# Layer 1 of a two-layer cross-attention: eleven of sixteen rotary chains transposed by VectorE in 32x32 blocks that DMA puts in place

## The chip, the cores and the metric

The kernel runs on one core of a Trainium2 chip. It is one launch in float32. The metric is the device time of the launch in microseconds (us): 2907.1 is the median of three runs (2905.81 to 2908.67).

A core has a TensorE (matrix products, results in PSUM), a VectorE, a ScalarE and a GpSimd (called PE, DVE, ACT and POOL in the profile), and SyncE (SP), which here only issues DMAs. Each engine works through its own queue in order, and waits on semaphores for the others.

## The reference

Four sequences of 1024 tokens with 512 features attend, twice, to a context of 1024 tokens with 384 features.

```python
# layer 0: 16 heads of 64
h = layernorm(x) * gamma + beta
Q, K, V = h @ Wq, context @ Wk, context @ Wv
x = x + (softmax(Q K^T) * 64**-0.5) V @ Wo + bo
# layer 1: 16 heads of 32
xn = x * rsqrt(mean(x * x) + 1e-5) * norm_w
q, k, v = xn @ wq, split(context @ wkv)
q, k = rotate(q, cos, sin), rotate(k, cos, sin)       # per head of 32
q, k = q / max(|q|, 1e-12), k / max(|k|, 1e-12)       # per head of 32
x = x + softmax(sqrt(32) * q k^T) v @ wout
```

The change is in layer 1 alone: in how the rotated and normalised q and k, made with tokens in partitions, come to have features in partitions, which the score product needs.

## The kernel before

The four sequences (batches) are worked one after the other. Layer 0 walks over eight pairs of heads; its softmax blocks are transposed by VectorE in 32x32 blocks (L401), and sixteen DMAs per block then put the 32-row bands in place (`regroup`, L407 to L413). Layer 1 works in two halves of eight heads, 256 features each. Each half has 32 steps of `Attention1.step` (L571): four query blocks of 256 tokens, two groups of four heads, four steps over the keys. A step makes scores for four heads and 256 keys on TensorE (L581), exponentials on ScalarE (L591), sums of exponentials on VectorE (L600, L602), and on TensorE the product of the step before with the values (L626). The denominators are added up by a product with ones in the second step of the next block (L645), and the quotient is formed by `divide` (L638, L639).

Queries and keys of layer 1 come from chains (`rotated_chains`, L452). A chain handles two tiles of 128 tokens and the 256 features of a half. Its three parts:

- `project` (L463): matmuls into a PSUM bank, 128 tokens by 256 features for each of the two tiles;
- `rotate` (L475), started by the last matmul: ScalarE squares the bank (L478), VectorE makes three products with cos and sin and adds them (L480 to L483), sums the squares per head (L485), and GpSimd makes the reciprocal norms and multiplies (L487 to L491). The result `t1` lies in one of four slots of a scratch tile, used in turn;
- `turn_over` (L494): four TensorE transposes of 128x128 into a PSUM bank (L499), and one ScalarE copy into the tile of q or k (L504).

Per batch there are sixteen chains: four each for k of half 0 (`k1_b_0`), q of half 0 (`q1_b_0`), k of half 1 and q of half 1. In this document q[0] to q[3] and k[0] to k[3] are those of half 0, and q1[0] to q1[3] and k1[0] to k1[3] those of half 1. All of k and q[0] are made before the steps of half 0 begin, and also k1[0] and the projection of k1[1]. The rest is woven between the steps of half 0: the units of a list are taken out by `Units.fill`, which spreads their costs (L828 to L859). In that list a chain's turn stands two places behind its projection (`weave`, lag 2), and `work.until(marks[n])` (L884) makes sure that q[1], q[2] and q[3] are turned before steps 8, 16 and 24, which read them first. The values of half 1 (`value_chains`, L536) are made in the same list. At the end of half 0 the rest of the list is emptied, so all of q1 and k1 is turned when half 1 begins at step 32. There the two loads of `wout` (L655) are issued by SP in program order, and after them the loads for the next batch; the first unit in step 32 is a product with `wout` (L165).

Both halves of the list run with matmuls that are split into four of 32 output columns once the steps have begun (`which["cols"]`, L832); in layer 0 they are split in two. PSUM banks for these units are given out in turn by `bank` (L127). A unit's cost (0.45 for a turn) only sets how the units are spread.

All loads and stores but three are issued by SP (`nc.sync`), in order. Each DMA uses one of eight semaphores in turn, and waits, before it is issued, for the DMA eight before it.

Of the kernel before, what the change touches and what calls it, by code (L numbers as in the profile page):

```python
# [30 lines left out]
AF = mybir.ActivationFunctionType  # L34
# [3 lines left out]
P = 128  # L38
S = 1024
NT = S // P  # L40
DQ = 512
NQ = DQ // P
DC = 384
NC_ = DC // P
# [4 lines left out]
HD1 = 32  # L49
NGRP = DQ // P  # L50
FH = DQ // 2
# [58 lines left out]
def xattn_kernel(ctx: ExitStack, tc: tile.TileContext, a: dict, out: bass.AP):  # L110
    nc = tc.nc
    x, c = a["x"], a["ctx_768"]
# [325 lines left out]
    TH = 2  # L438
# [10 lines left out]
        nc.sync.dma_start(wq, a["wq"][:, f0:f1].rearrange("(n p) m -> p n m", p=P))  # L449
        return wq  # L450

    def rotated_chains(dst, src, nk, w, name, tmp):  # L452

        hd, nh = HD1 // 2, TH * FH // HD1
        tiles = {}

        def heads(ap):
            return ap.rearrange("p (t h d) -> p t h d", t=TH, d=HD1)

        def spread(ap):  # L460
            return ap.unsqueeze(2).to_broadcast([P, TH, FH // HD1, ap.shape[2]])

        def project(t0, i, k):  # L463
            if i == 0 and k == 0:
                tiles[t0] = [bank(f"{name}_p{t0}")]
                if which["from"] == 0:
                    which["kept"] = which["n"]
            pp = tiles[t0][0]
            t = t0 + i
            lhsT = src[t // 4][:, k, (t % 4) * P : (t % 4 + 1) * P]  # L470
            matmul(pp[:, i * FH : (i + 1) * FH], lhsT, w(k), k == 0, k == nk - 1)
            if i == TH - 1 and k == nk - 1:
                rotate(t0, pp)

        def rotate(t0, pp):  # L475

            t1, t2, sq = tmp.take()
            nc.scalar.activation(sq, pp, AF.Square)  # L478
            c_, s_ = cos[:, t0 : t0 + TH, :], sin[:, t0 : t0 + TH, :]
            nc.vector.tensor_mul(heads(t1), heads(pp), spread(c_))  # L480
            nc.vector.tensor_mul(heads(t2)[:, :, :, :hd], heads(pp)[:, :, :, hd:], spread(s_[:, :, :hd]))
            nc.vector.tensor_mul(heads(t2)[:, :, :, hd:], heads(pp)[:, :, :, :hd], spread(s_[:, :, hd:]))
            nc.vector.tensor_add(t1, t1, t2)  # L483
            ss = sb.tile([P, nh], F32, tag="ss", bufs=2, name=f"{name}_s{t0}")
            nc.vector.tensor_reduce(ss, sq.rearrange("p (h d) -> p h d", d=HD1), AX.X, ALU.add)  # L485
# [5 lines left out]
            nc.gpsimd.tensor_mul(t1h, t1h, ri.unsqueeze(2).to_broadcast([P, nh, HD1]))  # L491
            tiles[t0] = t1

        def turn_over(t0):  # L494
            t1 = tiles.pop(t0)
            pt = bank(f"{name}_t{t0}")
            for g in range(2):
                for i in range(TH):
                    nc.tensor.transpose(  # L499
                        pt[:, (g * TH + i) * P : (g * TH + i + 1) * P],  # L500
                        t1[:, i * FH + g * P : i * FH + (g + 1) * P],
                        ident,
                    )
            nc.scalar.copy(dst()[:, :, t0 * P : (t0 + TH) * P], pt.rearrange("p (g t) -> p g t", g=2))  # L504

        return [
            (
                [(0.44, lambda t0=t0, i=i, k=k: project(t0, i, k)) for i in range(TH) for k in range(nk)],
                [],
                [(0.45, lambda t0=t0: turn_over(t0))],  # L510
            )
            for t0 in range(0, NT, TH)
        ]
# [19 lines left out]
            self.n += 1  # L533
            return self.t[:, self.n % 4], self.t[:, 4 + self.n % 2], self.t[:, 6 + self.n % 2]

    def value_chains(v, wv, ct, name):  # L536
        def one(t0, i, k, st={}):
            if i == 0 and k == 0:
                st["pp"] = bank(f"{name}_{t0}")
            t = t0 + i  # L540
            lhsT = ct[t // 4][:, k, (t % 4) * P : (t % 4 + 1) * P]
            matmul(st["pp"][:, i * FH : (i + 1) * FH], lhsT, wv[:, k, :], k == 0, k == NC_ - 1)
# [10 lines left out]
    WQ = 256  # L553

    class Attention1:
# [61 lines left out]
        def product(self):  # L617
# [15 lines left out]
            if end:  # L633
# [2 lines left out]

                def divide():
                    nc.vector.reciprocal(s[:, 1, :], s[:, 1, :])  # L638
                    nc.vector.tensor_mul(o[g][:, qb * WQ : (qb + 1) * WQ], s[:, 0, :], s[:, 1, :])  # L639

                def sums():
                    for i in (par, 3):
# [85 lines left out]
    for b in range(B):  # L728
# [92 lines left out]
        begin("q")  # L821
        kT, qT = kq["k"], kq["q"]
        kT1, qT1 = qk_tile(f"k1_{b}_1"), sb.tile([P, 2, S], F32, tag="raw", bufs=1, name=f"q1_{b}_1")
        q = rotated_chains(lambda kq=kq: kq["q"], xnT, NQ, lambda k, wq=wq: wq[0][:, k, :], f"q1_{b}_0", tmp)
        k1 = rotated_chains(lambda kT1=kT1: kT1, ct, NC_, lambda k, wk1=wk1: wk1[0][:, k, :], f"k1_{b}_1", tmp)
        q1 = rotated_chains(lambda qT1=qT1: qT1, xnT, NQ, lambda k: wq1[:, k, :], f"q1_{b}_1", tmp)

        work.add(flat(outs[:4]) + norms[0]["stats"] + k1[0][0] + [(AV, att.product)] + norms[0]["apply"])  # L828
        work.add(norms[0]["turn"] + q[0][0] + k1[1][0] + k1[0][2] + [(AV, att.product)] + flat(outs[4:]) + q[0][2])
# [14 lines left out]
        for half in range(2):  # L844
            n = 0
            if half == 0:
                vs = value_chains(att1.v1, wv1, ct, f"pv1_{b}_1")
                first = [q[1], (norms[1]["stats"], [], []), vs[0], (norms[1]["apply"], [], k1[1][2]), k1[2]]
                rest = [(norms[1]["turn"] + q[2][0], [], q[2][2]), k1[3], q[3], q1[0], vs[1], q1[1], q1[2]]
                rest += [q1[3], vs[2], vs[3]]  # L850
# [91 lines left out]
```

## Time and profile before

| | |
|---|---|
| median of three runs | 2907.1 us (2905.81 to 2908.67) |
| the profiled execution, its own time | 2903.3 us |
| its span | 2901.5 us |
| granted TensorE clock, mean | 0.999 |
| layer 1 half 0, first batch (steps 0 to 31) | 497 to 624 us of the span |
| layer 1 half 1, first batch (steps 32 to 63) | 624 to 755 us |
| TensorE transposes of the chains (L499) | 256, median 273 ns each, pipelined |
| ScalarE copies behind them (L504) | 64, some 590 ns each |

The profile is one execution, taken by the hardware profiler. Its page gives the busy time of each engine, the chain of work that ended last, and the groups of instructions by source line. Other views give an engine's instructions in order of time, merged where equal ones follow each other, with the idle time before them and what ended it in brackets; one line's instructions with their least, median and greatest durations in ns; and busy times in chosen stretches. Times in such rows are us from the span's start. A matmul of the source appears as two in the profile. `SPq` is SP's queue of DMA issues; a wait in it stands in the time of the issue.

### The profile page before, as it was taken

What the parts mean: (1) busy time and instruction counts of PE and PEld (TensorE: products, weight loads), DVE (VectorE), ACT (ScalarE), POOL (GpSimd) and SP (SyncE); (2) the same over time, 40 slices, a digit from 0 to 9 for tenths busy, and PEclk for the clock granted to TensorE, in tenths of its full rate; (3) what the DMA queues carried; (4) which work ended last, traced back from release to release, by engine and by line L of the source; (5) the groups of instructions that cost most, each with busy time, mean ns of one, the idle gap of its engine ahead of it and who ended that gap; (6) DMA issues with size and microseconds to landing.
All of it is one profiled execution on the core that took longest, in us unless ns stands there. A gap on an engine that the chain in (4) does not pass through costs nothing.

```text
span 2901.5 us, 66687 instructions
## 1 busy us (share of the span) xinstructions
PE 2849.7 (98%) x27336; PEld 1425.7 (49%) x27336; DVE 2189.1 (75%) x2952; ACT 1439.5 (50%) x2329; POOL 938.9 (32%) x776
## 2 busy tenths in 40 slices
PE   8999999999999999999999999999999999999998
PEld 4444455555444444555544445455554444445544
DVE  5677785877777778587777777858877777786877
ACT  4444444666444444466644444446664444444665
POOL 2343353420134335432024433534102343353400
PEclk9999999999999999999999999999999999999999
DMA  5887775010398777401039887730104887773000
GB/s 144 189 187 181 167 171 133 22 37 25 75 210 192 183 170 175 113 22 36 26 92 211 192 184 166 178 93 22 36 26 112 207 197 183 165 171 81 2 2 30
DMA packets 177552, 348.87 MB, mean 120 GB/s; under 512 B 37600, under 2 KB 93152, under 8 KB 177248
## 3 DMA queue, kind: packets, MB, share of 16 engines
q1 hardware_dynamic: 175920, 343.96, 50.1%
q8 instruction: 216, 3.54, 0.5%
q14 instruction: 88, 0.72, 0.1%
q10 hardware_dynamic: 1328, 0.66, 0.1%
HBM read 67.64 MB, written 8.39 MB: 26 GB/s over the span
## 4 chain that ended last, share of the span: by engine, by line
PE 89%; DVE 4%; ACT 3%; issue 2%; SPq 1%; DMA 1%; POOL 1%; DVEq 0%; ACTq 0%
PE s L367 16%; PE av L428 15%; PE po L165 11%; PE s L581 9%; PE pv L165 8%; PE pqT L165 7%; PE av L626 7%; PE pkT L165 5%; PE q_p L165 4%; PE k_p L165 2%; PE av L645 2%; ACT e L591 1%; SPq L412 1%; PE pth L247 1%; DMA eT<-e 1%
## 5 line engine op out<-in xcount | busy, mean ns | idle before, releaser
L392 DVE TENSOR_REDUCE m<-s 128x1 f32<-128x1024 f32 x512 | 602.9, 1219 | 372.1 <-PE s L367 371.5
L591 ACT ACTIVATE e<-s 128x1024 f32<-128x1024 f32 x512 | 496.7, 1022 | 252.5 <-PE s L581 239.5
L398 POOL TENSOR_SCALAR raw<-raw,li 128x1024 f32<-128x1024 f32 x256 | 287.1, 1122 | 725.0 <-DVE li L397 717.0
L367 PE MATMUL s<-qk 64*128 64x512 f32 x2048 | 515.6, 615 | 2.9 <-ACT e L393 2.2
L393 ACT ACTIVATE e<-s,m 128x1024 f32<-128x1024 f32 x256 | 283.1, 1110 | 465.8 <-DVE m L392 224.2
L393 ACT ACTIVATE raw<-s,m 128x1024 f32<-128x1024 f32 x256 | 285.4, 1115 | 455.0 <-DVE m L392 455.0
L428 PE MATMUL av<-eT,v 128*64 128x256 f32 x4096 | 470.1, 382 | 4.8 <-DMA eT<-e 3.6
L398 POOL TENSOR_SCALAR e<-e,li 128x1024 f32<-128x1024 f32 x256 | 287.0, 1122 | 473.7 <-DVE li L397 244.2
L600 DVE TENSOR_TENSOR both<-e 128x512 f32<-128x512 f32 x512 | 340.5, 699 | 87.2 <-ACT e L591 84.3
L428 PEld LDWEIGHTS av<-eT,v 128*64 128x64 f32 x4096 | 284.7, 137 | 225.1 <-issue 84.8
L367 PEld LDWEIGHTS s<-qk 64*128 64x128 f32 x2048 | 183.7, 186 | 281.6 <-issue 165.9
L581 PE MATMUL s<-q,k 32*128 32x256 f32 x4096 | 306.0, 401 | 5.8 <-ACT q L504 2.7
L401 DVE STREAM_TRANSPOSE e<-e 128x1024 f32<-128x1024 f32 x256 | 310.0, 1229 | 0.3
L401 DVE STREAM_TRANSPOSE e<-raw 128x1024 f32<-128x1024 f32 x256 | 310.0, 1228 | 0.2 <-DMA eT<-e 0.2
L581 PEld LDWEIGHTS s<-q,k 32*128 32x128 f32 x4096 | 192.1, 184 | 141.0 <-ACT e L591 72.0
L165 PE MATMUL pqT<-hT,w 128*64 128x512 f32 (+1 forms) x1216 | 240.6, 595 | 2.5 <-ACT hT L249 2.5
L165 PE MATMUL po<-wo,vals 128*64 128x512 f32 x1024 | 234.6, 596 | 0.0
L295 DVE TENSOR_TENSOR x<-x,po 128x512 f32<-128x512 f32 x200 | 131.7, 678 | 86.2 <-PE po L165 85.2
L165 PEld LDWEIGHTS pv<-w,cT 128*64 128x64 f32 (+1 forms) x3360 | 170.3, 132 | 41.6 <-issue 34.8
L165 PE MATMUL pv<-w,cT 128*64 128x128 f32 (+1 forms) x3360 | 184.3, 274 | 0.7 <-ACT hT L249 0.7
L165 PE MATMUL pkT<-cT,w 128*64 128x512 f32 (+1 forms) x912 | 182.4, 598 | 0.0
L602 DVE TENSOR_TENSOR both<-both 128x1024 f32<-128x1024 f32 x128 | 159.7, 1248 | 4.4
(82 smaller groups left out, 2776.1 us busy)
## 6 DMA issues: line engine op xcount, KB each, us to landing
eT<-e SPq DMA_DIRECT2D x2048, 128.0 KB, 2.4
xr<-in_x_dram SPq DMA_DIRECT2D x32, 256.0 KB, 4.0
wo<-in_Wo_dram SPq DMA_DIRECT2D x16, 512.0 KB, 4.5
x<-in_x_dram SPq DMA_DIRECT2D x32, 256.0 KB, 4.0
out_dram<-x SPq DMA_DIRECT2D x32, 256.0 KB, 2.6
w<-in_Wq_dram SPq DMA_DIRECT2D x31, 256.0 KB, 3.2
c<-in_ctx_dram SPq DMA_DIRECT2D x32, 192.0 KB, 4.2
wkv<-in_wkv_dram SPq DMA_DIRECT2D x16, 384.0 KB, 3.5
```

The source lines that it names most:

```text
L165: nc.tensor.matmul(o[rr], lhsT[:, rr], rhs, start=start, stop=stop)
L367: nc.tensor.matmul(sc[j][:, kb * 512 : (kb + 1) * 512], pr["qT"][r[j], i * P : (i + 1) * P], pr["kT"][r[j], kb * 512 : (kb + 1) * 512], st ...
L392: nc.vector.tensor_reduce(m[:, j : j + 1], sc[j], AX.X, ALU.max, negate=True)
L393: nc.scalar.activation(e[j], sc[j].rearrange("p (g s) -> p g s", g=4), AF.Exp, bias=m[:, j : j + 1], accum_out=l[:, j : j + 1])
L398: nc.gpsimd.tensor_scalar(e[j], e[j], li[:, j : j + 1], HD0**-0.5, ALU.mult, ALU.mult)
L401: self.turn = [lambda j=j: nc.vector.transpose(self.e[:, :, i % BQ * 2 + j, :], e[j]) for j in range(2)]
L428: nc.tensor.matmul(av[r[j], :W].rearrange("p (t a i) -> p t a i", t=BQ, a=4), pr["v"][:, k, r[j]], eT[:, j, :, :, k * 32 : (k + 1) * 32], ...
L581: nc.tensor.matmul(sc[j // 2][:, j % 2, c, :], kT[rr, g, k * P : (k + 1) * P], qT[rr, g, qb * WQ : (qb + 1) * WQ], start=True, stop=True,)
L591: nc.scalar.activation(e, sc[u], AF.Exp, scale=float(np.sqrt(np.float32(HD1))))
L600: nc.vector.tensor_add(into[:, 2 * u : 2 * u + 2, :], es[u][:, :, 0, :], es[u][:, :, 1, :])
L602: nc.vector.tensor_add(acc, acc, into)
L626: nc.tensor.matmul(self.av[rr, 0, :], v[g][:, 2 * kk + c, rr], es[j // 2][:, j % 2, c, :], start=first and c == 0, stop=end and c == 1,)
```

## The change

Eleven of a batch's sixteen chains (q[1] to q[3], k1[0] to k1[3], q1[0] to q1[3]) get another last part, `turn_blocks`, in place of `turn_over`. VectorE transposes `t1` (128x512) in place, each 32x32 block by itself, and SP issues sixteen DMAs: one for each 32-token band and each of the four heads of a group, of 32 partitions with two runs of 64 elements (256 bytes), 16 KB in all.

So that a run holds 64 elements, `rotate` writes these chains with the order head, tile, feature instead of tile, head, feature. The tokens of a pair of tiles then come to lie in the tile of q or k as: 32 tokens of the first tile, 32 of the second, the next 32 of the first, and so on. Keys of half 1 are in that order, so the values of half 1 are made in the same order, each of the four 32-column matmuls taking another 32 tokens of the context (`blocks=True`). Queries are in that order except for the first 256 of half 0, so `divide` puts tokens back when it writes the quotient. `turn_blocks` is entered in the list of units at cost 0. Nothing else changes; the loads keep their place in the program.

```diff
-    def rotated_chains(dst, src, nk, w, name, tmp):
+    def rotated_chains(dst, src, nk, w, name, tmp, dma_from=NT):
...
-        def heads(ap):
-            return ap.rearrange("p (t h d) -> p t h d", t=TH, d=HD1)
+        def heads(ap, t0=-1):
+
+            order = "p (h t d) -> p t h d" if t0 >= dma_from else "p (t h d) -> p t h d"
+            return ap.rearrange(order, t=TH, d=HD1)
...
-            nc.scalar.activation(sq, pp, AF.Square)
+            nc.scalar.activation(heads(sq, t0), heads(pp), AF.Square)
...
+            h1, h2 = heads(t1, t0), heads(t2, t0)
+            nc.vector.tensor_mul(h1, heads(pp), spread(c_))
+            nc.vector.tensor_mul(h2[:, :, :, :hd], heads(pp)[:, :, :, hd:], spread(s_[:, :, :hd]))
+            nc.vector.tensor_mul(h2[:, :, :, hd:], heads(pp)[:, :, :, :hd], spread(s_[:, :, hd:]))
...
+        def turn_blocks(t0):
+            t1 = tiles.pop(t0)
+            nc.vector.transpose(t1, t1)
+            to = dst()[:, :, t0 * P : (t0 + TH) * P].rearrange("p g (a c) -> p a g c", a=4)
+            for a in range(4):
+                rows = t1[32 * a : 32 * (a + 1)].rearrange("p (g h c) -> p h g c", g=2, h=4)
+                for h in range(4):
+                    nc.sync.dma_start(to[32 * h : 32 * (h + 1), a], rows[:, h])
...
-                [(0.45, lambda t0=t0: turn_over(t0))],
+                [(0.0, lambda t0=t0: turn_blocks(t0)) if t0 >= dma_from else (0.45, lambda t0=t0: turn_over(t0))],
...
-    def value_chains(v, wv, ct, name):
+    def value_chains(v, wv, ct, name, blocks=False):
...
+            if blocks:
+                for j in range(4):
+                    n0 = (t0 % 4 + j % TH) * P + (4 * i // TH + j // TH) * 32
+                    rr = slice(j * 32, (j + 1) * 32)
+                    nc.tensor.matmul(o[rr], ct[t // 4][:, k, n0 : n0 + 32], wv[:, k, :], start=k == 0, stop=k == NC_ - 1)
...
-                    nc.vector.tensor_mul(o[g][:, qb * WQ : (qb + 1) * WQ], s[:, 0, :], s[:, 1, :])
+                    to, num, den = o[g][:, qb * WQ : (qb + 1) * WQ], s[:, 0, :], s[:, 1, :]
+                    if half or qb:
+                        to = to.rearrange("p (t a x) -> p a t x", t=TH, a=4)
+                        num, den = (y.rearrange("p (a t x) -> p a t x", t=TH, a=4) for y in (num, den))
+                    nc.vector.tensor_mul(to, num, den)
...
-        q = rotated_chains(lambda kq=kq: kq["q"], xnT, NQ, lambda k, wq=wq: wq[0][:, k, :], f"q1_{b}_0", tmp)
-        k1 = rotated_chains(lambda kT1=kT1: kT1, ct, NC_, lambda k, wk1=wk1: wk1[0][:, k, :], f"k1_{b}_1", tmp)
-        q1 = rotated_chains(lambda qT1=qT1: qT1, xnT, NQ, lambda k: wq1[:, k, :], f"q1_{b}_1", tmp)
+        q = rotated_chains(lambda kq=kq: kq["q"], xnT, NQ, lambda k, wq=wq: wq[0][:, k, :], f"q1_{b}_0", tmp, TH)
+        k1 = rotated_chains(lambda kT1=kT1: kT1, ct, NC_, lambda k, wk1=wk1: wk1[0][:, k, :], f"k1_{b}_1", tmp, 0)
+        q1 = rotated_chains(lambda qT1=qT1: qT1, xnT, NQ, lambda k: wq1[:, k, :], f"q1_{b}_1", tmp, 0)
...
-                vs = value_chains(att1.v1, wv1, ct, f"pv1_{b}_1")
+                vs = value_chains(att1.v1, wv1, ct, f"pv1_{b}_1", True)
```

More of the change, by code (lines that the diff above doesn't have):

```diff
@@ L477, in rotate @@
             t1, t2, sq = tmp.take()
-            nc.scalar.activation(sq, pp, AF.Square)
+            nc.scalar.activation(heads(sq, t0), heads(pp), AF.Square)
             c_, s_ = cos[:, t0 : t0 + TH, :], sin[:, t0 : t0 + TH, :]
-            nc.vector.tensor_mul(heads(t1), heads(pp), spread(c_))
-            nc.vector.tensor_mul(heads(t2)[:, :, :, :hd], heads(pp)[:, :, :, hd:], spread(s_[:, :, :hd]))
-            nc.vector.tensor_mul(heads(t2)[:, :, :, hd:], heads(pp)[:, :, :, :hd], spread(s_[:, :, hd:]))
+            h1, h2 = heads(t1, t0), heads(t2, t0)
+            nc.vector.tensor_mul(h1, heads(pp), spread(c_))
+            nc.vector.tensor_mul(h2[:, :, :, :hd], heads(pp)[:, :, :, hd:], spread(s_[:, :, :hd]))
+            nc.vector.tensor_mul(h2[:, :, :, hd:], heads(pp)[:, :, :, :hd], spread(s_[:, :, hd:]))
             nc.vector.tensor_add(t1, t1, t2)
@@ L541, in one @@
             lhsT = ct[t // 4][:, k, (t % 4) * P : (t % 4 + 1) * P]
-            matmul(st["pp"][:, i * FH : (i + 1) * FH], lhsT, wv[:, k, :], k == 0, k == NC_ - 1)
+            o = st["pp"][:, i * FH : (i + 1) * FH]
+            if blocks:
[3 more added lines that the diff above has]
+                    nc.tensor.matmul(o[rr], ct[t // 4][:, k, n0 : n0 + 32], wv[:, k, :], start=k == 0, stop=k == NC_ - 1)
+            else:
+                matmul(o, lhsT, wv[:, k, :], k == 0, k == NC_ - 1)
             if i == TH - 1 and k == NC_ - 1:
```

## The prediction

> **What bounds the kernel now.** I read the page first, for who is the bound and whose work ends the span.
>
> ```profile
> span 2901.5 us, 66687 instructions
> PE 2849.7 (98%) x27336; PEld 1425.7 (49%) x27336; DVE 2189.1 (75%) x2952; ACT 1439.5 (50%) x2329; POOL 938.9 (32%) x776
> PE 89%; DVE 4%; ACT 3%; issue 2%; SPq 1%; DMA 1%; POOL 1%; DVEq 0%; ACTq 0%
> ```
>
> TensorE is busy 98% and is 89% of the chain that ended last: work taken from it is time gained, and a wait put in front of it is time lost. Next the stage table for half 0 of layer 1 in the first batch (columns: us, then busy time and count of PE, PEld, DVE, ACT, POOL; granted clock; DMA share; GB/s).
>
> ```profile
> 497.00:627.00 130.00, 126.08 (x1952) 70.41 (x1956) 103.62 (x144) 85.42 (x120) 47.20 (x29) 1.00 0.06 17
> ```
>
> TensorE has 4 us free in 130, VectorE 26; the DMA engines are nearly idle. Then TensorE in order of time there.
>
> ```profile
> 515.67 0.66 PE L499 MATMUL q_t<-ident,rot 128*128 128x128 f32 x4 [1.43 <-POOL rot L491]
> ...
> 558.41 0.66 PE L499 MATMUL q_t<-ident,rot 128*128 128x128 f32 x4
> 558.99 1.15 PE L581 MATMUL s<-q,k 32*128 32x256 f32 x16
> ...
> 562.36 1.15 PE L581 MATMUL s<-q,k 32*128 32x256 f32 x16
> ...
> 593.10 1.15 PE L581 MATMUL s<-q,k 32*128 32x256 f32 x16
> ...
> 626.30 1.90 PE L165 MATMUL po<-wo,o 128*32 128x512 f32 x16
> ```
>
> A turn occupies TensorE 0.58 us (558.41 to 558.99). Scores of steps 16 and 24 start at 562.36 and 593.10; they are the first to read q[2] and q[3]. At 626.30, in step 32, is the first product with `wout`. Last, SP's queue (a line's min/median/max ns; issues, KB each and us to landing; order of time), and under it VectorE in order of time with its block transpose.
>
> ```profile
> L412 SPq DMA_DIRECT2D eT<-e x2048: 507/589/2327, 47.3 to 2629.1; - x187
> eT<-e SPq DMA_DIRECT2D x2048, 128.0 KB, 2.4
> wo<-in_wout_dram SPq DMA_DIRECT2D x8, 512.0 KB, 4.2
> 477.84 18.96 SPq L655 DMA_DIRECT2D wo<-in_wout_dram  x2
> ```
>
> ```profile
> 541.47 0.68 DVE L485 TENSOR_REDUCE q_s<-rot 128x16 f32<-128x512 f32 x1
> ...
> 547.18 0.68 DVE L480 TENSOR_TENSOR rot<-k_p,cos 128x512 f32<-128x512 f32 x1
> L401 DVE STREAM_TRANSPOSE e<-e x256: 1220/1234/1247, 44.8 to 2616.4; 128x1024 f32<-128x1024 f32 x128
> ```
>
> A DMA costs SP half a microsecond and lands 2.4 us later; today the `wout` loads are issued 130 us before use, since SP has nothing else here.
>
> **Part 1: turns removed.** 11 chains x 4 batches = 44 turns x 0.585 us = 25.7 us of TensorE. ACT's copies (0.59 us each) and one PSUM bank per chain go too; ACT is half idle, so nothing, at most the 2.7 us that scores wait for that copy in the whole run. The 1.43 us wait for POOL at 515.67 goes as well: by then 0.6 + 1.4 = 2.0 us are won per batch.
>
> **Part 2: added on VectorE.** One 128x512 block transpose per chain, half of the 1234 ns row: 0.62 us. Ten of them are 6.2 us of half 0's 26 free; only their place in the queue counts, below. The rotation and Square write in runs of 32 instead of 512. No row shows that; the sin multiplies work in runs of 16 already at 0.41 us per 256 elements, against 0.69 per 512 for cos, so at most 0.14 us an operation and at least nothing. The same holds for the reordered quotient. I take nothing: VectorE's idle time hides it, and without that cover 0.14 x 4 lands on a chain's latency. Value projections already run as four 32-column matmuls here, and still do: nothing.
>
> **Part 3: added on SP.** Sixteen DMAs of 16 KB per chain, 704 in all. Nearest row, same queue, SBUF to SBUF, 32 partitions: 507 to 589 ns. Those carry 128 KB and come in bursts, so I take the low end, plus 0.04 us between two: 0.55 us. A batch of sixteen holds SP 8.8 us and is complete 15 x 0.55 + 2.4 = 10.65 us after its first issue. Ends for the range: 0.41 us (the `Wk` load issues at 0.37) and 0.63 (spacing in eT bursts).
>
> **Part 4: what waits.** In the changed kernel's instruction order, VectorE's transpose of q[2] stands behind the whole rotation of q[3], whose projection TensorE ends only just before step 16; and step 16's scores wait for its sixteen DMAs. Times of the first batch (in all four the first `wout` product comes 2.55 us after q1[3]'s turn, so I take four times the same), VectorE 2.0 us earlier than before:
> - k1[1]: reduce ends 540.1, transpose 540.7, landed 551.4. The rotation of k1[3], ready at 547.18 - 2.0 + 0.6 = 545.8, writes over its scratch and so waits 5.6 us. Behind it on VectorE stand k1[2]'s transpose and the sums of steps 12 to 14.
> - Rotation (547.18 to 549.77) 2.6: 554.0; transpose of k1[2] 554.6; SP until 563.4.
> - VectorE: six sums (3 x 1.3 the pair), two accumulations (1.2 each), the division (2.2), together 8.5: 563.1; rotation of q[3] 565.7; transpose of q[2] 566.3; issued until 575.1, landed 577.0. Step 16 was at 562.36: **14.6 us later**.
> - k1[3]'s transpose stands after q1[0]'s rotation (ended 573.3) and two sums, 574.5 + 0.6 + 14.6 = 589.7: SP until 598.5; q[3], ready before, queues behind it, landed 609.2. Step 24 would be 593.10 + 14.6 - 3 turns (1.75) = 605.95: 3.2 more. Sum 16.05.
> - q1[1]'s stands after q1[3]'s rotation (ended 611.6) and two sums, 612.9 + 16.05 = 629.0: SP until 637.8; q1[2] until 646.6, q1[3] until 655.4, each ready while the one ahead is issuing. The `wout` load stands behind them in SP's order: landed 655.4 + 4.2 = 659.6. TensorE wants it at 626.30 + 16.05 - 1.75 = 640.6: a wait of 19.0 us, now 33.3 behind. The next batch's `c` loads follow on SP eight issues later, 3.8 us, and land 4.1 us after that, 663.3; their transposes come 4.8 us after TensorE resumes, at 664.4: covered, barely.
>
> Less k1[0]'s turn (0.6) that is 32.7 per batch, x 4 = 130.8.
>
> **Part 5: TensorE after a long wait.** Its order of time at the start:
>
> ```profile
> 9.70 4.12 PE L165 MATMUL pkT<-cT,w 128*64 128x512 f32 x12
> ...
> 15.21 2.80 PE L165 MATMUL pkT<-cT,w 128*64 128x512 f32 x12
> ...
> 105.44 3.67 PE L428 MATMUL av<-eT,v 128*64 128x256 f32 x32 [2.50 <-DMA eT<-e]
> ```
>
> Twelve matmuls soon after the first data take 1.3 us more than the same twelve later, both at a granted clock of 1.00; after 2.50 us idle nothing is slower (3.67, as at 89.69). I take the first for waits above 10 us; the ends are 0 and 1.3. Two waits per batch above 10 us, 1.3 us each, x 4 = 10.6.
>
> [...]
>
> [...]
>
> **Sum.** The profiled execution took 2903.3 us around the span of 2901.5, and lies 3.8 below the median of 2907.1. 2903.3 + 130.8 + 10.6 = 3044.7, so 3045.
>
> **Rivals.**
> - *Light issue.* Same mechanism at 0.41 us per DMA: step 16 is 10.4 late, step 24 adds nothing, the `wout` load leaves 19.2 - 0.6 = 18.6 per batch: +74, with the clock 2988. For: small transfers on an idle fabric. Against: the 507 minimum.
> - *Heavy issue.* 0.63 us: 41.5 per batch, +166, 3080; at 0.80 (pieces of 256 B, which no row has) 60.9 per batch, +244, 3158.
> - *Only step 16 pays.* The `wout` load does not queue: 14.6 + 3.2 - 6.4 = 11.4 per batch, +46, 2954. Against: it stands behind q1[3] in SP's order.
> - *Faster.* The DMAs are hidden and only the turns count: 2903.3 - 25.7 - 5.7 = 2872. This needs the losses under 7.9 us per batch, that is an issue of about 0.18 us. The lowest on SP is 0.33 (a `c` load).
> - *Not done.* Excluded: the built order has 176 fewer transposes on TensorE.
>
> **How the numbers follow.** Forecast 0.55, light 0.22, heavy 0.14, only step 16 0.06, faster 0.03. The range 2970 to 3110 holds the first two and heavy up to some 0.69 us, leaving out the last two and half of heavy. A measurement of this kernel tells 0.2% (6 us) from no change; only *faster* lies below, and the unforeseen gets 0.01 for no change.
>
> **What would show it.** TensorE waiting about 15 us on DMA before step 16's scores and 19 us before the first `wout` product, four times each; SP issuing almost without pause from q1[1] on; VectorE stopped about 5 us before k1[3]'s rotation; 2 us less TensorE work per batch before that. Wrong if the new DMAs issue far from 0.55 us or land far from 2.4.

## The result, and the profile after

The changed kernel takes 3142.3 us (median of four runs, 3137.29 to 3145.57) against 2907.9 us for the kernel before: 1.080 times the time, with a 95% interval of 1.0786 to 1.0813. The forecast of 3045 had the direction and the places right and the size too small; the time lies outside the range of 2970 to 3110. The profiled execution took 3137.29 us and spans 3135.4, that is 233.9 more than the profile before.

The first lines of the page of the changed kernel, and its chain of work that ended last by engine:

```profile
span 3135.4 us, 67329 instructions
PE 2889.9 (92%) x27160; PEld 1445.6 (46%) x27160; DVE 2215.3 (71%) x2996; ACT 1419.2 (45%) x2285; POOL 922.0 (29%) x776
PE 75%; SPq 9%; DVE 7%; DMA 4%; ACT 3%; issue 3%; DVEq 0%; ACTq 0%
```

Read the second line against the one before. TensorE has 176 matmul records fewer, and its busy time has *risen* by 40.2 us (2849.7 to 2889.9). The rest of the 233.9 is idle time: 245.5 us of the span now against 51.8 (span less busy), 193.7 more. SP's queue, 1% of the chain before, is 9%. Two things have to be explained: new waits, and the same matmuls taking longer.

The waits, in TensorE's order of time of the first batch (start, duration, engine, line, operation, output and inputs, shape, count; in brackets the idle time before and what ended it). The functions of the change have moved down by some lines: L605 is the scores, L166 the projections.

```profile
561.78 2.99 PE L605 MATMUL s<-q,k 32*128 32x256 f32 x16 [5.27 <-ACT e L615]
...
582.13 3.90 PE L605 MATMUL s<-q,k 32*128 32x256 f32 x16 [13.95 <-DMA q<-rot]
...
589.85 1.15 PE L605 MATMUL s<-q,k 32*128 32x256 f32 x16
...
620.78 3.92 PE L605 MATMUL s<-q,k 32*128 32x256 f32 x16 [5.88 <-DMA q<-rot]
...
681.87 3.64 PE L166 MATMUL po<-wo,o 128*32 128x512 f32 x16 [24.14 <-DMA wo<-in_wout_dram]
```

These are steps 15, 16, 17 and 24 and the first product with `wout` in step 32. All four batches show the same four waits. Over the run, `wout` is waited for 96.8 us, q 78.8, and step 15 some 22. The wait of step 15 is put down to ScalarE, but begins on VectorE, which could not start k1[3]'s rotation until k1[1]'s DMAs had read the scratch tile. VectorE in order of time:

```profile
543.89 0.70 DVE L514 STREAM_TRANSPOSE rot<-rot 128x512 f32<-128x512 f32 x1
...
556.73 0.69 DVE L486 TENSOR_TENSOR rot<-k_p,cos 128x512 f32<-128x512 f32 x1 [7.64 <-DMA k<-rot]
...
571.78 0.70 DVE L514 STREAM_TRANSPOSE rot<-rot 128x512 f32<-128x512 f32 x1
```

The first line is k1[1]'s block transpose, the second the rotation that stands 7.64 us, the third q[2]'s transpose, 9.4 us after the time at which step 16 began in the kernel before (562.36). Then SP's queue in order of time:

```profile
572.50 10.17 SPq L519 DMA_DIRECT2D q<-rot  x16
599.76 10.72 SPq L519 DMA_DIRECT2D k<-rot  x16
610.62 67.14 SPq L519 DMA_DIRECT2D q<-rot  x80
677.80 1.10 SPq L683 DMA_DIRECT2D wo<-in_wout_dram  x2
```

Sixteen DMAs hold SP 10.2 us and more. The 80 in the third line are q[3] and all four of q1, with a pause of 14 us in them (q1[1] is transposed at 644.78 us). The `wout` loads, issued at 477.84 us before, are issued at 677.80, behind all of them. The line's durations (least, median, greatest in ns) and the page's time to landing:

```profile
L519 SPq DMA_DIRECT2D q<-rot x448: 585/595/1715, 517.4 to 3005.9; - x150
```

```profile
q<-rot SPq DMA_DIRECT2D x448, 16.0 KB, 1.8
```

The issue time is that of `eT` (median 589 ns), though a DMA carries 16 KB instead of 128. With the gap to the next it is 0.64 us (10.17 / 16). It lands 1.8 us later, so a DMA's wait for the one eight before it (8 x 0.64 = 5.1 us) is not what sets this pace.

Now the longer matmuls. The scores of step 16 take 3.90 us, those of step 17 1.15. The stage table in stretches of 1 us (columns as in the table shown of before; the granted clock is the third figure from the end):

```profile
557.00:560.00 3.00, 0.00 (x0) 0.00 (x0) 2.97 (x7) 0.00 (x0) 0.43 (x2) 1.00 0.00 0
560.00:561.00 1.00, 0.00 (x0) 0.00 (x0) 1.00 (x3) 0.29 (x1) 1.00 (x1) 0.59 0.00 0
...
566.00:567.00 1.00, 1.00 (x16) 0.54 (x12) 0.90 (x2) 0.79 (x1) 0.00 (x0) 0.50 0.13 24
567.00:568.00 1.00, 1.00 (x24) 0.40 (x16) 1.00 (x2) 0.60 (x1) 0.00 (x0) 1.00 0.17 32
...
570.00:571.00 1.00, 0.00 (x0) 0.00 (x0) 0.97 (x3) 0.00 (x0) 0.00 (x0) 0.71 0.09 16
...
582.00:583.00 1.00, 0.87 (x3) 0.78 (x4) 0.00 (x0) 0.00 (x0) 0.00 (x0) 0.50 0.17 33
583.00:584.00 1.00, 1.00 (x7) 0.74 (x5) 0.00 (x0) 0.00 (x0) 0.00 (x0) 0.50 0.09 16
584.00:585.00 1.00, 1.00 (x11) 0.91 (x10) 0.00 (x0) 0.00 (x0) 0.00 (x0) 0.50 0.00 0
...
587.00:588.00 1.00, 1.00 (x20) 0.45 (x15) 0.71 (x2) 0.37 (x2) 0.00 (x0) 0.76 0.00 0
588.00:589.00 1.00, 1.00 (x24) 0.59 (x20) 0.00 (x0) 0.21 (x1) 0.00 (x0) 1.00 0.00 0
...
628.00:629.00 1.00, 1.00 (x20) 0.54 (x16) 0.00 (x0) 0.00 (x0) 0.00 (x0) 0.78 0.09 16
```

TensorE goes idle at 556.5, before step 15, and the clock is halved from 560.2, 3.7 us later. It is back at 1.00 from 567.0, 5.2 us after step 15 began. TensorE goes idle again at 568.2, before step 16, and the clock is halved from 570.4, 2.2 us later. When work returns at 582.13, it stays at 0.50 for another 5.4 us, until 587.5; behind the wait before step 24 (620.78) it stays so for 7.7 us, until 628.4. The tail behind a wait is therefore paid in matmuls that nobody delays any more: step 17 begins 7.72 us after step 16, where it was 4.67 before; step 25 8.86 us after step 24 instead of 4.48.

### The profile page after: what moved, and what is told of

Its sections match the earlier page's. It is cut to its first block, busy times and chain, and to the rows that moved or that the text cites. A ratio compares the mean times of both kernels' runs of the same rounds, so it can differ in the third digit from the quotient of the medians.

```text
span 3135.4 us, 67329 instructions
## 1 busy us (share of the span) xinstructions
PE 2889.9 (92%) x27160; PEld 1445.6 (46%) x27160; DVE 2215.3 (71%) x2996; ACT 1419.2 (45%) x2285; POOL 922.0 (29%) x776
## 4 chain that ended last, share of the span: by engine, by line
PE 75%; SPq 9%; DVE 7%; DMA 4%; ACT 3%; issue 3%; DVEq 0%; ACTq 0%
PE s L368 14%; PE av L429 13%; PE po L166 10%; PE s L605 7%; SPq L519 7%; PE pqT L166 6%; PE pv L166 6%; PE av L650 5%; PE pkT L166 5%; PE k_p L166 2%; PE q_p L166 2%; SPq L413 2%; PE av L673 2%; ACT e L615 2%; DVE both L624 2%
## 5 line engine op out<-in xcount | busy, mean ns | idle before, releaser
L605 PE MATMUL s<-q,k 32*128 32x256 f32 x4096 | 343.3, 414 | 108.8 <-DMA q<-rot 78.8
L605 PEld LDWEIGHTS s<-q,k 32*128 32x128 f32 x4096 | 216.2, 190 | 258.7 <-issue 117.2
L166 PE MATMUL pqT<-hT,w 128*64 128x512 f32 (+1 forms) x1216 | 242.2, 598 | 2.5 <-ACT hT L250 2.5
L166 PE MATMUL po<-wo,vals 128*64 128x512 f32 x1024 | 234.6, 596 | 0.0
L166 PE MATMUL po<-wo,o 128*32 128x512 f32 (+1 forms) x824 | 131.2, 630 | 99.7 <-DMA wo<-in_wout_dram 96.8
L166 PEld LDWEIGHTS pv<-w,cT 128*64 128x64 f32 (+1 forms) x3360 | 170.4, 132 | 41.5 <-issue 34.8
L166 PE MATMUL pv<-w,cT 128*64 128x128 f32 (+1 forms) x3360 | 184.3, 274 | 0.7 <-ACT hT L250 0.7
L166 PE MATMUL pkT<-cT,w 128*64 128x512 f32 (+1 forms) x912 | 181.6, 596 | 0.0
```

Source lines behind the costliest of these rows:

```text
L166: nc.tensor.matmul(o[rr], lhsT[:, rr], rhs, start=start, stop=stop)
L605: nc.tensor.matmul(sc[j // 2][:, j % 2, c, :], kT[rr, g, k * P : (k + 1) * P], qT[rr, g, qb * WQ : (qb + 1) * WQ], start=True, stop=True,)
```

## The experiments

Theory A is that of the prediction: SP's price per DMA and its program order set the losses, at three places (VectorE's blocked rotation, step 16, the `wout` load). The rivals are named with each run. Diffs are against the changed kernel, and show the lines that matter. The kernel before, timed again beside each group of runs, took 2911.2 to 2912.8 us, and 2907.9 beside the changed kernel, so differences of some 5 us between groups mean nothing.

**q alone.** q[1] to q[3] by blocks, k1, q1 and the values of half 1 as in the kernel before.

```diff
-        k1 = rotated_chains(lambda kT1=kT1: kT1, ct, NC_, lambda k, wk1=wk1: wk1[0][:, k, :], f"k1_{b}_1", tmp, 0)
-        q1 = rotated_chains(lambda qT1=qT1: qT1, xnT, NQ, lambda k: wq1[:, k, :], f"q1_{b}_1", tmp, 0)
+        k1 = rotated_chains(lambda kT1=kT1: kT1, ct, NC_, lambda k, wk1=wk1: wk1[0][:, k, :], f"k1_{b}_1", tmp)
+        q1 = rotated_chains(lambda qT1=qT1: qT1, xnT, NQ, lambda k: wq1[:, k, :], f"q1_{b}_1", tmp)
...
-                vs = value_chains(att1.v1, wv1, ct, f"pv1_{b}_1", True)
+                vs = value_chains(att1.v1, wv1, ct, f"pv1_{b}_1")
```

> Only q[1], q[2] and q[3] are turned by VectorE and DMA; k1, q1 and the values of half 1 are as before the change. Theory A (SP's queue: every chain holds SP some 10.2 us, and the loss is where TensorE waits for the end of that queue, plus a slow stretch of TensorE after each long wait): the wait for wout is gone, since no q1 chain stands ahead of it; step 24 has 16 us of room and does not wait; step 16 still waits, about 11 us, and runs 3 us slow after it. Some 14 us per batch lost, 2908 + 56 = about 2964. Theory B (VectorE: its queue blocked by the scratch that DMA still reads, and the added transposes, make the loss): no chain here reuses scratch that DMA still reads, so little is lost, 2900 to 2920.

Measured: 2960.7 us, 1.0161 (1.0140 to 1.0181). The only new wait that comes in each batch is the one before step 16:

```profile
571.40 3.92 PE L605 MATMUL s<-q,k 32*128 32x256 f32 x16 [9.84 <-DMA q<-rot]
```

It is 9.78 to 9.84 us in each batch, with the same long scores behind it. Three chains are enough to lose 1.6%, with only 48 DMAs per batch added on SP: q[2]'s transpose still stands behind q[3]'s rotation on VectorE, and sixteen issues and a landing follow. Theory A holds.

**Half 1 alone.** k1 and q1 by blocks, q as before.

```diff
-                    if half or qb:
+                    if half:
...
-        q = rotated_chains(lambda kq=kq: kq["q"], xnT, NQ, lambda k, wq=wq: wq[0][:, k, :], f"q1_{b}_0", tmp, TH)
+        q = rotated_chains(lambda kq=kq: kq["q"], xnT, NQ, lambda k, wq=wq: wq[0][:, k, :], f"q1_{b}_0", tmp)
```

> Only k1 and q1 (eight chains per batch) are turned by VectorE and DMA; q[1] to q[3] as before the change. Theory A: no waits before steps 16 and 24; q1[1], q1[2] and q1[3] still queue on SP ahead of the wout load, so TensorE waits some 18 to 22 us for it and runs 2 us slow after it; gain 8 turns x 0.585 = 4.7 us. Some 15 to 20 us per batch lost, 2908 + 60 to 80 = 2968 to 2988. Theory B: the rotation of k1[3] still waits some 7 us on VectorE for k1[1]'s DMAs and stops TensorE some 5 us in step 15, and that is most of it: under 2930.

Measured: 3035.4 us, 1.0418 (1.0398 to 1.0439), above both expectations. The waits of the first batch:

```profile
558.32 2.99 PE L605 MATMUL s<-q,k 32*128 32x256 f32 x16 [4.84 <-ACT e L615]
...
652.35 3.64 PE L166 MATMUL po<-wo,o 128*32 128x512 f32 x16 [24.23 <-DMA wo<-in_wout_dram]
```

I had put the rotation blocked on VectorE under the rival only. It is there (7.64 us in the first batch) beside the `wout` wait, which is as long as with q's DMAs (24.23 against 24.14), since three batches of q1 stand ahead of the load in either case. Together the two lose more (234 us) than apart (48 and 123): the rest is 63, or 16 per batch. Most of it lies at steps 16 and 24, for which the two share SP: 4.1 us more at the one (13.95 for 9.84), 5.88 and a tail of 4.4 at the other, where neither part alone waits.

**The loads moved ahead.** The `wout` loads, and the next batch's first three weight loads and four of its eight `c` loads, are issued before step 17 and no longer at step 32.

```diff
...
+                    if half == 0 and n == 17:
+                        wo1 = [wo_load(a["wout"], i, f"wo1_{b}_{i}") for i in range(2)]
+                        adds = add_units(xt, lambda n: o[n], lambda n: wo1[0][:, n % 2, :], f"po1_{b}_0", (0, 1))
+                        if b + 1 < B:
+                            st, order = prepare_units(b + 1)
+                            first, later = order(adds)
+                            first[0][1]()
+                            first[1][1]()
```

> The changed kernel, with the two wout loads and the next batch's first nine loads issued before step 17 instead of at step 32. Theory A: the wait of 24 us for wout and 2 us of slow TensorE after it are gone, four times: 3142 - 106 = about 3036; the loads hold SP some 4 us between the chains, so step 24 may wait 0 to 4 us longer, up to 3052. Theory B: unchanged within 30 us, since TensorE would then wait for VectorE instead.

Measured: 3086.1 us, 1.0594 (1.0574 to 1.0613). That is some 34 us above the upper end expected. The wait for `wout` is gone, and another load in the same queue takes its place:

```profile
682.78 0.99 PE L192 MATMUL ptc<-ident,c 128*128 128x128 f32 x2 [11.22 <-DMA c<-in_ctx_dram]
```

SP issues c[4] to c[7] at 680.22 us, still behind q1. Moving one load past the queue frees it; what stays behind is late next. In the prediction I had the `c` loads as covered, barely; that was so only while the `wout` wait was ahead of them.

**Half as many DMAs.** Eight per chain, of 64 partitions and 32 KB each; the bytes are the same. The blocks do not land where the scores need them, so this run is read for its times alone.

```diff
-                rows = t1[32 * a : 32 * (a + 1)].rearrange("p (g h c) -> p h g c", g=2, h=4)
-                for h in range(4):
-                    nc.sync.dma_start(to[32 * h : 32 * (h + 1), a], rows[:, h])
+                rows = t1[64 * (a // 2) : 64 * (a // 2 + 1)].rearrange("p (g h c) -> p h g c", g=2, h=4)
+                for h in range(2):
+                    nc.sync.dma_start(to[64 * h : 64 * (h + 1), a], rows[:, 2 * (a % 2) + h])
```

> The changed kernel with eight DMAs of 64 partitions and 32 KB per chain in place of sixteen of 32 partitions and 16 KB: as many bytes, and the blocks land in other places than the computation needs. Theory A, with a price per DMA: a chain holds SP 5.1 us; step 16 comes some 8 us earlier, the wait before step 24 goes with its slow stretch (some 10 us), the wait for wout falls from 24 to 8 us: 34 us per batch, about 3005. If the price goes by bytes: 3142 still. Theory B: the wait of k1[3]'s rotation shortens by 5 us, no more than 20 to 30 us in all.

Measured: 2999.4 us, 1.0298 (1.0273 to 1.0323); 143 us less than the changed kernel, and close to what the price per DMA gives. The line's durations:

```profile
L519 SPq DMA_DIRECT2D q<-rot x224: 590/605/1757, 516.6 to 2867.1; - x112
```

A DMA of 32 KB costs SP 605 ns, one of 16 KB 595: here the price was per DMA, not per byte. The wait for `wout` falls from 24.1 to 9.7 us, that of step 24 goes, and the one of step 16 is 12.3.

**Six slots for `t1`.** The scratch tile has six slots for the rotated features and one each for the other two uses, so k1[3] does not write where k1[1]'s DMAs still read.

```diff
-            return self.t[:, self.n % 4], self.t[:, 4 + self.n % 2], self.t[:, 6 + self.n % 2]
+            return self.t[:, self.n % 6], self.t[:, 6], self.t[:, 7]
```

> The changed kernel with six slots for a chain's result instead of four (one each for the other two scratch rows), so that no rotation waits for DMAs that still read its slot. Theory A (SP's queue): the 5 us wait in step 15 goes and step 16 comes some 5 us earlier, the rest stays, because k1[1], k1[2] and q[2] still queue on SP one behind the other: some 6 us per batch, 3142 - 25 = about 3117. Theory B (VectorE): the loss falls by more than 60 us.

Measured: 3117.0 us, 1.0704 (1.0687 to 1.0720), as theory A said. Step 15's wait goes; step 16 waits 16.35 us instead of 13.95, and `wout` 24.18 as before. The blocked rotation is a real but small term, 25 us in all; SP's queue takes back part of it.

**The chain's turn one place earlier.** Lag 1 instead of 2 in the list, and the marks that go with it.

```diff
-                work.add(weave(chains, 2))
+                work.add(weave(chains, 1))
-                    return sum(len(x[0]) for x in chains[: i + 3]) + sum(len(x[2]) for x in chains[: i + 1])
+                    return sum(len(x[0]) for x in chains[: i + 2]) + sum(len(x[2]) for x in chains[: i + 1])
```

> The changed kernel with every turn one place behind its projection in the list instead of two, so that each chain's DMAs are issued some 7 to 11 us earlier; count of DMAs and of work as in the changed kernel. SP's queue: k1[1], k1[2] and q[2] then end at about 565 where step 16 wants them at 560, step 24 does not wait, the wout load lands some 7 us late instead of 24: about 9 us per batch lost, 2908 + 36 = 2944, between 2925 and 2970. If the loss were in VectorE's work or in the DMAs as such, it would stay above 3100.

Measured: 3014.8 us, 1.0354 (1.0337 to 1.0371): 127 us less than the changed kernel, about two thirds of what I expected, and outside its range. The waits above 1 us in layer 1 of the first batch:

```profile
520.12 1.81 PE L673 MATMUL av<-both,ones 128*32 128x256 f32 x16 [3.14 <-ACT rest L659]
...
570.00 3.91 PE L605 MATMUL s<-q,k 32*128 32x256 f32 x16 [6.09 <-DMA q<-rot]
...
624.80 1.23 PE L673 MATMUL av<-both,ones 128*32 128x256 f32 x8 [1.94 <-DVE both L624]
...
652.92 3.64 PE L166 MATMUL po<-wo,o 128*32 128x512 f32 x16 [13.07 <-DMA wo<-in_wout_dram]
```

VectorE's order is a large part of the loss at step 16: the transposes stood behind whole rotations that were not needed yet. But an earlier transpose stands in front of the sums, and waits of 3.14 and 1.94 us appear there; and SP's 10.2 us per chain stay.

**Is the tail TensorE's clock?** Unread matmuls keep TensorE busy before step 16, step 24 and the first `wout` product: 12, 5 and 22 units of four.

```diff
+        def keep_busy(units, name):
+            pp = bank(f"busy_{b}_{name}")
+            for i in range(units):
+                matmul(pp, ident, bo, True, True)
...
+                    if half == 0 and n in (16, 24):
+                        keep_busy(12 if n == 16 else 5, n)
...
```

> The changed kernel with matmuls added that nothing reads, at the places where TensorE waits for DMA: 48 (of 32 columns by 512) before step 16, 20 before step 24, 88 before the first wout product, per batch. They fill some 11 of 14, 5 of 6 and 21 of 24 us of these waits and take nothing from SP or VectorE. If the slow stretches behind the waits come from TensorE's clock after idling, they go, some 3, 4.4 and 2.3 us per batch, and the granted clock rises: 3142 - 39 = about 3103, though TensorE does more. If they come from anything else (the DMAs' writes, a pipeline that refills), 3142 or some us more.

Measured: 3144.5 us, 1.0799 (1.0783 to 1.0816), level with the changed kernel; but it tells the theories apart badly, because the filler ended before the wait did. Of the three waits 3.69, 2.91 and 5.96 us were left, and the clock was halved behind each (mean 0.67 from 582 to 590 us, 0.50 from 626 to 631, 0.61 from 682 to 690). The shortest:

```profile
625.90 3.92 PE L605 MATMUL s<-q,k 32*128 32x256 f32 x16 [2.91 <-DMA q<-rot]
```

```profile
625.00:626.00 1.00, 0.10 (x1) 0.13 (x1) 0.00 (x0) 0.00 (x0) 0.00 (x0) 0.88 0.17 32
626.00:627.00 1.00, 1.00 (x3) 0.87 (x4) 0.00 (x0) 0.00 (x0) 0.00 (x0) 0.50 0.09 18
```

So the next run has 7 units before step 15, and 18, 9 and 31 at the other three places.

> Unread matmuls again, but enough of them to last until the awaited transfer has landed: 7 units of four before the scores of step 15, 18 before step 16, 9 before step 24, 31 before the first wout product. Nothing else is changed, so every transfer lands when it did. Theory A (the long tails behind the waits are TensorE at a lower clock after idle time): granted clock 0.95 or more from 566 to 690 us, scores of steps 16 and 24 in 1.2 us instead of 3.9, first wout product 1.9 instead of 3.6; the tails that go are 3.0 + 4.4 + 2.3 us per batch, the fillers overrun by some 1 to 2 us per batch: 3105 to 3118. Rival (the tails are work that was held up and would be late anyway): clock near 1.00 but 3140 or more.

Measured: 3146.4 us, 1.0801 (1.0786 to 1.0815). The clock part came as theory A has it: 1.00 in every stretch from 582 to 750 us (0.89 from 566 to 582, after a filler had to wait), and the tails are gone.

```profile
573.01 17.35 PE L166 MATMUL busy<-bo,ident 128*32 128x512 f32 x144 [4.56 <-DVE rot L488]
590.30 1.15 PE L605 MATMUL s<-q,k 32*128 32x256 f32 x16
...
627.45 2.35 PE L605 MATMUL s<-q,k 32*128 32x256 f32 x16
...
687.40 1.90 PE L166 MATMUL po<-wo,o 128*32 128x512 f32 x16
```

The time part did not: 3146 is the time of the rival. The fillers overran more than I had allowed. In the changed kernel step 16 begins 9.6 us after q[2]'s first issue (572.50 to 582.13); here that issue is at 574.83, so the step could have begun at 584.5 and began 5.8 later. In the same way step 24 is 1.3 late and the `wout` product 1.7 late: 8.8 us per batch lost to overrun, against 9.8 of tails (3.05 + 4.4 + 2.3). The scores and the other four groups of layer 1 that stood in slow stretches are busy 782.2 us here and 833.8 in the changed kernel (318.9, 137.0, 126.1, 125.1 and 75.1 against 343.3, 147.3, 134.6, 131.2 and 77.4), 51.6 less with the same matmuls. At the `wout` product, which reads no heads, the clock alone makes the tail: 3.64 us in the changed kernel at 0.50, 1.90 here at 1.00. At steps 16 and 24 two things stretch the scores together, the clock and heads that land one after another; step 24's take 2.35 us here at a clock of 1.00. As an estimate, half of the time at half rate behind the three waits is 2.7 + 3.8 + 2.3 = 8.8 us, so most of the 9.8 is the clock. That taking the tails away would shorten the run by as much is only worked out.

The part that is not the clock can be seen at step 8. Its scores take 2.95 us in the changed kernel at a clock of 1.00: its four heads land 0.64 us apart, and 3 x 0.64 = 1.9 us is about the 1.8 by which they are longer than 1.15.

**Is there a version that gains?** First k1 alone, where the keys are read only in half 1 and SP has time.

```diff
-        q = rotated_chains(lambda kq=kq: kq["q"], xnT, NQ, lambda k, wq=wq: wq[0][:, k, :], f"q1_{b}_0", tmp, TH)
+        q = rotated_chains(lambda kq=kq: kq["q"], xnT, NQ, lambda k, wq=wq: wq[0][:, k, :], f"q1_{b}_0", tmp)
-        q1 = rotated_chains(lambda qT1=qT1: qT1, xnT, NQ, lambda k: wq1[:, k, :], f"q1_{b}_1", tmp, 0)
+        q1 = rotated_chains(lambda qT1=qT1: qT1, xnT, NQ, lambda k: wq1[:, k, :], f"q1_{b}_1", tmp)
```

(With six slots, and the quotient as before; these lines are not shown.)

> Only the four k1 chains are turned by VectorE and DMA, with six slots; q[1] to q[3] and q1 as before the change. SP is free again by about step 20 and has no chain ahead of the wout load; nothing reads k1 before step 32. Theory A: no wait is left, and 16 turns of 0.585 us are won: 2908 - 9 = 2899, 0.3% faster. Theory B: VectorE's additional work alone makes it slower than before.

Measured: 2907.9 us against 2911.2, 0.9991 (0.9982 to 1.0000). TensorE waits for none of the new DMAs, and 3 us of the 9.4 of the turns arrive, hardly clear of no gain. Against them stands a new wait for VectorE, 2.11 us in each batch:

```profile
553.01 1.23 PE L670 MATMUL av<-both,ones 128*32 128x256 f32 x8 [2.11 <-DVE both L624]
...
1271.41 1.23 PE L670 MATMUL av<-both,ones 128*32 128x256 f32 x8 [2.11 <-DVE both L624]
1272.57 1.91 PE L605 MATMUL s<-q,k 32*128 32x256 f32 x16
```

```profile
1273.00:1274.00 1.00, 1.00 (x16) 0.70 (x8) 1.00 (x3) 0.05 (x1) 1.00 (x1) 0.50 0.17 33
```

These 8.4 us are more than what is missing; other waits became shorter, so the account does not close. In the second batch (the lower lines) the clock is halved behind the same wait (0.50, scores in 1.91 us) that leaves it at 1.00 in the first; the scores behind it take 1.15 us in the first, third and fourth.

Then some of q1 as well, with `dma_to` as an upper bound in `rotated_chains`, the loads ahead of step 17 and six slots: q1[0] to q1[2], and q1[0] and q1[1].

```diff
-        q1 = rotated_chains(lambda qT1=qT1: qT1, xnT, NQ, lambda k: wq1[:, k, :], f"q1_{b}_1", tmp, 0)
+        q1 = rotated_chains(lambda qT1=qT1: qT1, xnT, NQ, lambda k: wq1[:, k, :], f"q1_{b}_1", tmp, 0, 6)
...
```

> Seven chains per batch by blocks: k1[0] to k1[3] and q1[0] to q1[2]; q[1] to q[3] and q1[3] by TensorE as before; the wout loads and the next batch's w pair and first c loads are issued ahead of step 17, and t1 has six slots. Theory A (TensorE loses only what waits for a DMA that SP has not issued in time): SP has 7 x 10.2 = 71 us of issuing in the 130 us of half 0, and nothing behind it that is wanted soon, so no wait on a DMA of q, k, wout or c above 1 us. Then 28 turns x 0.585 = 16.4 us go, less what the run with k1 alone lost to VectorE (6 us in all for 16 turns, up to 10 for 28): 6 to 11 us under the kernel before. Rival (VectorE's added transposes and reordered quotients set the time of this stage themselves): waits on VectorE of 4 us or more per batch, and no gain or a loss (0 to +20).

> As the run with seven chains, but q1[2] by TensorE too: six chains by blocks, 61 us of issuing per batch. Theory A (SP's queue decides): if the run with seven chains still waits for q1[2] or for loads behind it, this one does not, and it is 4 to 9 us under the kernel before (24 x 0.585 = 14.0, less 6 to 9 lost to VectorE). Rival (VectorE decides): about half way between the run with k1 alone and the run with seven chains, whichever way that one went.

Measured on one chip, against 2912.8 us there: seven chains 2907.1 us, 0.9978 (0.9969 to 0.9988), six chains 2900.7 us, 0.9955 (0.9942 to 0.9969). Both gain. The seven miss the lower edge of my range by little; the six gain 12 us where I expected 4 to 9. The waits for the `c` loads are 8.3 us in the run with seven and 6.4 with six (6.2 before), so the seventh chain costs a little on SP; where the rest of the 6 us between them lies is open. The 2.11 us wait for VectorE is not in either. Whether the loads that were moved or the fifth and sixth chain removed it wasn't tried.

Last, q[1] by blocks in addition to the six, since SP is idle when it is made.

```diff
-        q = rotated_chains(lambda kq=kq: kq["q"], xnT, NQ, lambda k, wq=wq: wq[0][:, k, :], f"q1_{b}_0", tmp)
+        q = rotated_chains(lambda kq=kq: kq["q"], xnT, NQ, lambda k, wq=wq: wq[0][:, k, :], f"q1_{b}_0", tmp, TH, 2 * TH)
...
```

> The run with six chains, and q[1] of half 0 by blocks as well: its sixteen DMAs are issued from about 520 to 530 us, when SP has nothing else, and step 8 reads q[1] only at about 532. Theory A (a chain costs nothing where SP is free and there is time before its reader): no wait on DMA at step 8 above 1 us, and the 1.0 us wait of TensorE for GpSimd ahead of q[1]'s turn goes in each batch: 4 x (0.585 + 1.0) = 6.3 us less than the run with six chains, so 18 us (14 to 20) under the kernel before on the same chip. Rival (VectorE, with one more transpose and reordered quotient, holds up the sums): a wait on VectorE or on ScalarE of 1.5 us or more per batch takes its place, and the run is level with the one with six chains, 12 us under, or worse.

Measured: 2907.8 us, 0.9988 (0.9978 to 0.9998): the rival. TensorE's wait for GpSimd goes, as expected, and the wait for VectorE is back:

```profile
551.58 1.23 PE L673 MATMUL av<-both,ones 128*32 128x256 f32 x8 [2.11 <-DVE both L624]
```

The scores of step 8 are 1.88 us instead of 1.15 too, as heads land one after another. Six chains are the best version found: 0.45% faster than the kernel before.

## Why the prediction was wrong, point by point

**Bound, parts 1 and 2: right.** TensorE was the bound, and the records of turns fell by 176. The wait for GpSimd ahead of q[1]'s turn went over to VectorE (1.49 us before the transpose at 516.66). A block transpose takes 0.70 us for the 0.62 taken. The rotation's five operations take what they took (0.69, 0.41, 0.41, 0.69, 0.68), so writing in runs of 32 costs nothing that shows. TensorE did get ahead: step 14 begins at 553.07 us for 555.47 before, although layer 0 ended 1.4 us later. The clock again accounts for about as much: behind a wait of 2.15 us in layer 0 it was halved from 106.2 to 109.6 us, and the product there took 5.36 us for the 3.67 of the kernel before:

```profile
105.89 5.36 PE L429 MATMUL av<-eT,v 128*64 128x256 f32 x32 [2.15 <-DMA eT<-e]
```

**Part 3 failed: the price of a DMA on SP.** I took 0.55 us, from the least of the nearest row (507 ns) plus 0.04, arguing that 16 KB is lighter than 128. It is 0.595 + 0.04, 0.64, which is the term of the sum that was too small, and the run with eight DMAs per chain shows why the argument was wrong: the price did not follow the bytes (605 ns for 32 KB). The median of that row, 589 ns, was the number to take. The landing of 1.8 instead of 2.4 us gives back 0.6 per batch of sixteen; it is complete after 15 x 0.64 + 1.8 = 11.4 us for the 10.65 forecast.

**Part 4: places right, sizes short.** All four places came, in all four batches: VectorE stopped before k1[3]'s rotation (7.64 us for 5.6), waits before step 16 (13.95, and 5.27 already in step 15, 19.2 together for some 15), SP issuing without a pause over q1[1] to q1[3] (645.51 to 677.80, 32.3 us for 26.4), the first `wout` product behind them (24.14 for 19.0). In the times of the first batch:

- step 16 at 582.13 for 577.0: 5.1 late, 1.4 of it from layer 0. VectorE was not 2.0 us ahead, as I had it, though TensorE was: k1[1]'s transpose came at 543.89 for 540.1. It stands behind q[2]'s rotation, and q[2]'s projection, spread anew among the steps, ended at 540.6 for 538.8 before.
- step 24 at 620.78 for 609.2: 6.5 more. 3.05 are the slow tail behind step 16. k1[3]'s first DMA came another 1.9 later than forecast (17.6 us after step 16 began, for 12.7). SP took 3.4 more for k1[3] and q[3] (599.76 to 620.73, 21.0 for 17.6), but the scores began with the first head and not when the last had landed, 1.8 sooner than I had them: 1.6 net.
- the `wout` product at 681.87 for 659.6: 10.7 more. 5.9 are SP over q1, 4.4 the tail behind step 24.
- behind it another 2.3 of tail.

**Part 5 failed: TensorE after a long wait.** I took 1.3 us for each of two waits per batch, from a row with a granted clock of 1.00 beside it. In the changed kernel the clock rows do show the loss, at 0.50 behind all four long waits of a batch, not two, and the three tails named above are 9.8 us per batch for 2.6 (the one behind step 15 lies in front of the wait of step 16 and costs nothing). My row, twelve matmuls near the start of the run, was by my estimate the same thing cut short. The trace's list of clock changes begins at 12.41 us, and a row before that prints 1.00 for want of an entry; half rate up to there, which no row shows, would cost (12.41 - 9.70) / 2 = 1.36 us, about the 1.3 that I read. The same twelve matmuls in the changed kernel and with q alone:

```profile
9.74 3.22 PE L166 MATMUL pkT<-cT,w 128*64 128x512 f32 x12
```

```profile
9.69 4.63 PE L166 MATMUL pkT<-cT,w 128*64 128x512 f32 x12
```

In the changed kernel the list begins at 10.64 us, which gives 2.80 + (10.64 - 9.74) / 2 = 3.25 us for the 3.22 of the row. A row of the start, 1.3 us in the kernel before, 0.4 in the changed one and 1.8 with q alone, was no measure of a wait: the half rate lasted 5.4 us at step 16, 7.7 at step 24 and 4.6 at `wout` (681.87 to 686.5), and half of these is 2.7, 3.8 and 2.3 us.

**The sum.** The profiled execution is 3137.3 - 3044.7 = 92.6 us above the forecast, 23.1 per batch. From the list: SP 1.6 + 5.9 = 7.5; k1[3]'s DMAs that start later 1.9; tails 9.8 - 2.6 = 7.2; the late start of step 16 5.1, with k1[0]'s turn, 0.6, that the first batch did not give: 5.7. That is 22.3; 0.8 stays unexplained, and this is the account of the first batch alone. With 0.64 us in its own working the prediction would have come to about 3084, and with the tails beside it to some 3113.

**The rivals.** *Heavy issue* was the case that came (0.64 for its 0.63), but its 3080 held only 2.6 us of tails per batch, and its 0.80 is shown by no run. *Light issue* fell by the 10.17 us of q[2] on SP, *only step 16 pays* by the `wout` load that was issued at 677.80, behind q1[3]. *Faster* had the right condition, a loss under 7.9 us per batch, and the six-chain version meets it by giving SP only what it has time for, not by a lower price per DMA.

## What to carry to other kernels

A transpose of 0.58 us on a full engine was replaced by sixteen DMAs that hold their queue for 10.2 us: count the issues, not the bytes, and take the median of the nearest row in the same queue as the price. Then ask which loads stand behind them in program order, and move those first. And read the granted clock behind every wait of TensorE, from 2 us on (it fell behind one of 2.15 us in the changed kernel): behind three waits of the first batch the matmuls ran 2.3 to 4.4 us longer here, beyond the wait itself, and the longest tail stood behind the shortest of the three (4.4 behind 5.88 us, 2.3 behind 24.14).

## What the runs showed of the hardware

- The SP price of a DMA from SBUF to SBUF was 589, 595 and 605 ns for 128, 16 and 32 KB, over 32, 32 and 64 partitions.
- In the changed kernel the granted clock changed only at marks that lie whole multiples of 3.41 us apart: in the first batch at 560.2, 567.0, 570.4, 587.5, 618.2, 628.4, 662.6 and 686.5 us. A stretch between two marks with 1.2 us of work in it was followed by half the clock (567.0 to 570.4), one with 2.0 us was not (655.8 to 659.2).
- The length of a wait alone did not tell whether the clock fell: it was 0.50 behind one of the four waits of 2.11 us with k1 alone, and behind the one of 2.15 us in layer 0 of the changed kernel; behind the other three the scores took 1.15 us, and behind one of 2.50 us in the kernel before it stayed at 1.00.
- After work returned behind the long waits of the changed kernel's first batch, the half rate lasted another 4.6 to 7.7 us.
- Sixteen DMAs that put four heads in place one after the other, band by band, release the heads 0.64 us apart; the scores that read all four were stretched by 1.8 us at a clock of 1.00 (2.95 for 1.15, step 8 of the changed kernel).
